# Two graph layers in one kernel: other block bounds, and the last two spans of each layer in an order of their own

## The chip, the core and the metric

The kernel runs on one core of one Trainium2 chip. The metric is the device time of one execution in microseconds (us), the median of five runs. A separate execution was taken with the hardware profiler. Engines are named as the profile names them: PE is TensorE (PEld its weight loads), DVE is VectorE, ACT is ScalarE, POOL is GpSimd, SP is SyncE, which here only issues DMAs. All data are float32.

## What is computed

There are N = 6250 nodes with D = 256 features and E = 106250 edges, sorted by destination; the last 6250 are the nodes' own loops. Each layer adds a per-edge message into the edge's destination and runs a small network on every node. The reference, cut to what matters (batch norm `_bn` and the weights are given as inputs):

```python
# layer 0
msg = relu(x[src] + edge_attr)
agg = segment_sum(msg, dst)
h = x + (x + agg)
f = gelu(_bn1(h) @ W1.T + b1) @ W2.T + b2
x = layernorm(x + _bn2(h + f))
# layer 1
m = gelu((x[src] + edge_attr) @ W1m + b1m) @ W2m + b2m
agg = segment_sum(m, dst) / max(deg, 1)
u = gelu(agg @ W1u + b1u) @ W2u + b2u
out = layernorm(x + _layer_norm(x + u, gamma, beta))
```

## The kernel before, in words

**Spans and blocks.** The edges are cut into 831 tiles of 128 (the last has 10), and eight tiles make a *span*: V = 104 spans, numbered 0 to 103, the last with seven tiles. A span has two groups of four tiles (`G = 4`), and a group two pairs. Nodes are cut into *blocks* of `SB = 256`: 25 of them, the last of 106. As the edges are sorted, a span touches a known range of nodes (`window[v]`, about 160 wide), so one or two blocks. `parts(v)` (L590) lists them, `first_span` and `last_span` say when a block opens and when it is full, and `shape(b)` (L604) gives its width, in how many halves H of n rows.

**Per span.** POOL gathers the source rows with one indirect DMA per tile (`gather`, L789) into one of five ring buffers (`RING = 5`, so POOL can run ahead until a ring is still in use). The edge rows are copied by ACT into PSUM (`lifted`, L825) and DVE adds them to the gathered ones (`add_to_gathered`, L833); ACT applies the function to a whole group (`activated`, L841). Each pair of tiles is then summed into 32 slots by matmuls with one-hot matrices made by DVE (`one_hots` L849, `into_slots` L868), ACT copies the slots out (`kept_slots` L884), and further matmuls with a second one-hot (`slot_nodes` L859) add them to the accumulator of the block (`into_blocks` L887).

**The product with W1m.** Layer 1 needs `edge_attr @ W1m`. PE turns a pair of tiles (`turned`, L800: transposes, then an ACT copy `eaT`) and multiplies them (`product`, L814). For the first group of each span this is done in layer 0, and the result stored to DRAM (`zst`, through the tile `z`, L1101 and L1110); layer 1 loads it in place of the edges. For the second group it is done in layer 1 (`load_1` L1237 loads its edges). The gathered table of layer 1 is not the node features but `proj`, their product with W1m, which the node part of layer 0 writes.

**Per block.** When a block is full its node part starts: a generator with stages, `nodes_0` (L972: batch norm, W1 and gelu, W2 with residual and statistics, normalization, transposes, projection and its write to `proj`) or `nodes_1` (L1170: mean, two halves of W1u and gelu, the residual's adds, W2u and statistics, first norm, second norm and output). `running` holds the generators under way and `advance` (L939) moves each by one stage. A norm's inverse root is an ACT square root and a DVE reciprocal (`inverted`, L959), and a square root and a gelu need different ACT tables. Every stage's PSUM comes from `node_work()` (L656), a pool with one buffer, `nodeP`; at the very end of a layer it takes `workP`, with four.

**The order.** The program is in manual schedule: each engine's queue holds its instructions in the order in which the code issues them. Step v (`step_0` L1080, `step_1` L1274) gathers span v, turns and multiplies, adds up span v-1, sums span v-2 into slots and span v-3 into blocks, and moves the generators by one stage each. After 104 steps `end_0` (L1114) or `end_1` (L1305) finishes what is left, with the last two blocks' generators moved together. Layer 1's first gather waits for every write to `proj`, since any edge may need any node. `end_0` also issues the first three spans' loads of layer 1 on SP, ahead of the last blocks' writes there.

## Time and profile before

| | us |
|---|---|
| median of 5 runs | 2770.07 |
| lowest and highest | 2761.28 and 2791.77 |
| the profiled execution | 2788.11 |
| its span, first to last instruction | 2786.2 |
| busy in it: PE, DVE, ACT, POOL | 2058.7, 1409.3, 1348.3, 1582.7 |
| last gather of layer 0 issued, first of layer 1 | 1311.1 and 1374.2 |
| last gather of layer 1 issued, end of the span | 2711.2 and 2786.2 |

A span's row in the list by order of time has: start, time, engine, line of the code, operation, what it writes and reads, shape, count, and in brackets how long the engine stood idle before it and what ended that. In the table by windows each row has the window, its length, then busy time (and count of instructions) of PE, PEld, DVE, ACT and POOL, the granted TensorE clock as a share of full speed, the DMA engines' share and GB/s. "remote" is a releaser that the profile could not name. Matmuls are pipelined and their ends are modelled.

### The profile page before, as it was taken

To read this page: it belongs to the slowest core of one execution; us is meant where nothing else is said; L and a number is where in the kernel's file an instruction comes from. 1 tells how busy PE (TensorE), PEld (TensorE's weight loads), DVE (VectorE), ACT (ScalarE), POOL (GpSimd) and SP (SyncE) were. 2 spreads that over 40 slices of the span, in tenths; PEclk is the share of its full clock that TensorE was granted. 3 is DMA by queue.
4 is the path that set the end of the run, shared out by engine and by line. 5 is a ranking of instruction groups with operands and counts; after the bars stand their busy time and mean duration, and the time that the engine had idled before them with its cause. 6 is when DMAs were issued, how large, how long until landed. Compare 5 with 4: busy or idle time off the path is not lost.

```text
span 2786.2 us, 37166 instructions
## 1 busy us (share of the span) xinstructions
PE 2058.7 (74%) x11784; PEld 1530.4 (55%) x11784; DVE 1409.3 (51%) x4130; ACT 1348.3 (48%) x2138; POOL 1582.7 (57%) x1671
## 2 busy tenths in 40 slices
PE   3778786788878878878726667776877678778786
PEld 2556565556655556656514555555655556555564
DVE  3545554455555555555313455444555546455455
ACT  1455554555555555555413444444454446445454
POOL 6565665566656656655255546555666566566550
PEclk7888998999999999999767888888999889898898
DMA  6677676667666767766445555555655456466550
GB/s 216 213 229 229 221 236 210 201 223 246 218 219 224 237 223 235 232 214 201 156 123 161 165 154 188 168 163 163 194 176 189 158 176 192 158 192 193 161 162 15
DMA packets 312069, 531.71 MB, mean 191 GB/s; under 512 B 36325, under 2 KB 231480, under 8 KB 311736
## 3 DMA queue, kind: packets, MB, share of 16 engines
q1 hardware_dynamic: 231416, 309.65, 33.5%
q0 software_dynamic: 79744, 217.71, 25.8%
q8 instruction: 97, 1.59, 0.2%
q10 hardware_dynamic: 704, 1.87, 0.2%
q14 instruction: 108, 0.88, 0.1%
HBM read 455.34 MB, written 73.75 MB: 190 GB/s over the span
## 4 chain that ended last, share of the span: by engine, by line
PE 20%; another core or an unknown queue 11%; issue 7%; DVE 6%; ACT 6%; DMA 2%; POOL 1%; ACTq 0%; SPq 0%; DVEq 0%; POOLq 0%
PE workP L819 8%; PE nodeP L1211 3%; PE acc L904 3%; PE slotP L876 2%; DVE ring L837 2%; ACT ring L845 2%; PE workP L806 2%; PE nodeP L1184 2%; DMA ring<-proj,src_sb 1%; DVE hot L854 1%; ACT workP L830 1%; ACT L961 1%; ACT eaT L811 1%; POOL ring L793 1%
## 5 line engine op out<-in xcount | busy, mean ns | idle before, releaser
L793 POOL DMA_INDIRECT ring<-proj,src_sb x831 | 790.6, 951 | 609.6 <-issue 275.2
L793 POOL DMA_INDIRECT ring<-in_x_dram,src_sb x831 | 790.2, 951 | 518.4 <-issue 257.6
L819 PE MATMUL workP<-w1m_sb,eaT 128*128 128x256 f32 x3324 | 891.7, 414 | 102.0 <-ACT eaT L811 67.7
L837 DVE TENSOR_TENSOR ring<-workP,ring 128x512 f32<-128x512 f32 x832 | 542.6, 683 | 562.5 <-remote 274.3
L819 PEld LDWEIGHTS workP<-w1m_sb,eaT 128*128 128x128 f32 x3324 | 653.3, 205 | 302.8 <-issue 91.1
L904 PE MATMUL acc<-hot,sums 128*128 128x160 f32 (+19 forms) x1360 | 268.3, 335 | 329.0 <-DVE hot L898 136.6
L845 ACT ACTIVATE ring<-ring 128x1024 f32<-128x1024 f32 x418 | 441.5, 1057 | 66.1 <-DVE ring L837 53.7
L904 PEld LDWEIGHTS acc<-hot,sums 128*128 128x128 f32 x1360 | 213.3, 220 | 372.5 <-ACT sums L885 124.4
L885 ACT COPY sums<-slotP 128x257 f32<-128x257 f32 (+1 forms) x208 | 77.2, 371 | 698.8 <-remote 355.0
L830 ACT COPY workP<-ea 128x512 f32<-128x512 f32 x624 | 343.5, 594 | 80.0 <-DVE ring L837 57.2
L811 ACT COPY eaT<-workP 128x512 f32<-128x512 f32 x416 | 230.4, 585 | 309.8 <-PE workP L806 127.2
L806 PE MATMUL workP<-ident,ea 128*128 128x128 f32 x1662 | 251.2, 286 | 143.6 <-DVE z L1101 71.2
L876 PE MATMUL slotP<-ring,hot 128*32 128x257 f32 (+1 forms) x3324 | 257.9, 407 | 77.3 <-remote 36.2
L806 PEld LDWEIGHTS workP<-ident,ea 128*128 128x128 f32 x1662 | 198.8, 146 | 204.0 <-DVE z L1101 92.5
L854 DVE TENSOR_SCALAR hot<-ramp,slot 128x32 f32<-128x32 f32 x1662 | 267.0, 260 | 0.0
L876 PEld LDWEIGHTS slotP<-ring,hot 128*32 128x32 f32 x3324 | 104.8, 113 | 201.3 <-issue 93.7
L1101 DVE COPY z<-workP 128x512 f32<-128x512 f32 x104 | 71.3, 686 | 198.4 <-PE workP L819 94.0
L917 DVE TENSOR_TENSOR degs<-degs,slotP 1x160 f32<-1x160 f32 (+24 forms) x170 | 36.3, 241 | 228.3 <-issue 89.1
L1194 ACT ACTIVATE uT<-uT,cols_sb 128x256 f32<-128x256 f32 (+1 forms) x100 | 44.6, 495 | 168.5 <-DVE uT L1189 128.6
L1110 DVE COPY z<-workP 128x512 f32<-128x512 f32 x104 | 71.4, 687 | 97.5 <-remote 48.1
L1184 PE MATMUL nodeP<-fT,w 128*128 128x256 f32 x368 | 97.8, 409 | 17.2 <-issue 8.5
L1211 PE MATMUL nodeP<-w2u_sb,uT 128*128 128x256 f32 x352 | 100.5, 450 | 0.0
(138 smaller groups left out, 1505.7 us busy)
## 6 DMA issues: line engine op xcount, KB each, us to landing
ea<-in_edge_attr_dram SPq DMA_DIRECT2D x103, 1024.0 KB
zst<-z SPq DMA_DIRECT2D x104, 512.0 KB
ea<-zst SPq DMA_DIRECT2D x104, 512.0 KB
ea<-in_edge_attr_dram SPq DMA_DIRECT2D x103, 512.0 KB
ring<-in_x_dram,src_sb POOLq DMA_INDIRECT x831
ring<-proj,src_sb POOLq DMA_INDIRECT x831
xb<-in_x_dram SPq DMA_DIRECT2D x24, 256.0 KB
x1d<-x SPq DMA_DIRECT2D x24, 256.0 KB
```

The costliest lines, as they stand in the source:

```text
L793: nc.gpsimd.indirect_dma_start(out=rings[v % RING][:n, g * G + j, :D], out_offset=None, in_=table, in_offset=bass.IndirectOffsetOnAxis(ap= ...
L806: nc.tensor.transpose(pe[:, j, k, :n], ea[:n, q + j, k * P : (k + 1) * P], ident[:n, :n])
L811: nc.scalar.copy(eaT[:, j:k, :, :n], pe[:, j:k, :, :n])
L819: nc.tensor.matmul(ph[:n, j, :], lhsT=eaT[:, j, k, :n], rhs=w1m_sb[:, k, :], start=(k == 0), stop=(k == KC - 1),)
L830: nc.scalar.copy(ps[:n, j:k, :], of[:n, q + j : q + k, :])
L837: nc.vector.tensor_add(r[:n, at + j : at + k, :D], ps[:n, j:k, :], r[:n, at + j : at + k, :D])
L845: nc.scalar.activation(at, at, func)
L854: nc.vector.tensor_scalar(hots[v][:n, j, :], ramp[:n, :SLOTS], slot[:n, t : t + 1], None, op0=ALU.is_equal,)
L876: nc.tensor.matmul(ps[q * SLOTS : (q + 1) * SLOTS, :width], lhsT=hot[:n, j, :], rhs=r[:n, j, :width], start=(i == 0), stop=(i == PAIR - 1 ...
L904: nc.tensor.matmul(acc[b][:, k, cols], lhsT=its[:, k * P : (k + 1) * P], rhs=at, start=(begins and k == 0), stop=(last_span[b] == v and k ...
L1184: nc.tensor.matmul(ps[:, o - i, :width], lhsT=w12[:, k, o * P : (o + 1) * P], rhs=mT[:, k, :width], start=(k == 0), stop=(k == KC - 1),)
L1211: nc.tensor.matmul(ps[:n, h, :], lhsT=uT[:, k, h * P : h * P + n], rhs=w2u_sb[:, k, :], start=(k == 0), stop=(k == UC - 1),)
```

## The change

It has six parts.

- **Bounds.** The blocks are no longer multiples of 256. The last two get 160 and 96 nodes (`LAST`), the first takes the rest of 106, and 23 of 256 lie between: 26 blocks. A block of 160 has two halves of 80 rows. Indices `b * SB` become `bounds[b]` throughout, and the halves' columns `h * P` become `h * n`.
- **The last two steps.** `step_0` and `step_1` run for spans 0 to 101. The last two (c and d in the code) are in `end_0` and `end_1`, with `advance(list(running))` at places of their own. The very last span is added, activated and summed into slots pair by pair (`arriving`), with a stage of every running generator between the pairs.
- **Products of the last spans.** Spans 102 and 103 have both groups multiplied in layer 0 (`stored_products`), in half-steps that `fill` places between the other work and, for the rest, after the last node part; the second groups go to a new DRAM tensor `zst1`, and layer 1 loads them from there. So layer 1 has no products for these two spans, and layer 0's last two steps have none in their usual place.
- **Banks and roots.** The last two blocks' stages take PSUM from `workP` or from the accumulators' pool, and their inverse root is a DVE add and a power on POOL (`inverted` with `last`).
- **Loads and gathers.** The source indices are loaded in two pieces, the first of 64 columns. A span's gathers are issued with the short tile first, and this tile, which has 10 edges, is gathered with 127 rows in layer 0 and 120 in layer 1. Two spans' loads of layer 1 are issued ahead of the last node parts, the third after them.
- **Small.** `invert` (the reciprocal of the degrees) is called at the end of `full_1` and no longer at the end of the step; code that was not used is gone.

The diff, cut to its core:

```diff
--- before.py
+++ after.py
...
+LAST = (160, 96)
...
+LATE = 2
+FIRST = 64
...
     c.update(
...
+    bounds = [0, (N - sum(LAST)) % SB]
+    while bounds[-1] < N - sum(LAST):
+        bounds.append(bounds[-1] + SB)
+    for width in LAST:
+        bounds.append(bounds[-1] + width)
+    if bounds[1] == 0:
+        bounds.pop(0)
+    blocks = len(bounds) - 1
     V = len(window)
 
     def parts(v):
 
         lo, hi = window[v]
         return [
-            (b, max(lo, b * SB), min(hi, (b + 1) * SB))
-            for b in range(lo // SB, (hi - 1) // SB + 1)
+            (b, max(lo, bounds[b]), min(hi, bounds[b + 1]))
+            for b in range(blocks)
+            if bounds[b] < hi and lo < bounds[b + 1]
         ]
...
     def shape(b):
 
-        width = min(SB, N - b * SB)
+        width = bounds[b + 1] - bounds[b]
         H = -(-width // P)
-        assert width == H * min(width, P)
-        return width, H, min(width, P)
+        assert width % H == 0
+        return width, H, width // H
 
     def rows_of(ap, b):
...
             return psw.tile([P, 2, D], F32, name="workP")
 
-        draining = []
-
         def node_work():
-            return work() if draining else psn.tile([P, 2, D], F32, name="nodeP")
+            return psn.tile([P, 2, D], F32, name="nodeP")
+
+        def acc_work():
+            return psa.tile([P, KC, SB], F32, name="acc")
 
...
 
-            nc.sync.dma_start(out=src_sb, in_=src)
+            nc.sync.dma_start(out=src_sb[:, :FIRST], in_=src[:, :FIRST])
+            nc.sync.dma_start(out=src_sb[:, FIRST:], in_=src[:, FIRST:])
...
 
-        def gather(v, table):
-            for g in range(GROUPS):
-                for j, n in enumerate(tiles_of(v, g)):
-                    t = v * SPAN + g * G + j
-                    nc.gpsimd.indirect_dma_start(
-                        out=rings[v % RING][:n, g * G + j, :D],
-                        out_offset=None,
-                        in_=table,
-                        in_offset=bass.IndirectOffsetOnAxis(ap=src_sb[:n, t : t + 1], axis=0),
-                    )
+        def gather(v, table, least=0):
+            counts = tiles_of(v, 0) + tiles_of(v, 1)
+
+            for j in sorted(range(len(counts)), key=lambda j: counts[j]):
+                t, n = v * SPAN + j, max(counts[j], least)
+                nc.gpsimd.indirect_dma_start(
+                    out=rings[v % RING][:n, j, :D],
+                    out_offset=None,
+                    in_=table,
+                    in_offset=bass.IndirectOffsetOnAxis(ap=src_sb[:n, t : t + 1], axis=0),
+                )
 
...
+        def activated_pair(v, g, q, func):
+            at = g * G + q
+            for j, k, n in runs(tiles_of(v, g)[q : q + 2]):
+                r = rings[v % RING][:n, at + j : at + k, :D]
+                nc.scalar.activation(r, r, func)
+
...
+        def slots_of(v, width, ps, its):
+
+            hot, r = hots[v], rings[v % RING]
+            counts = tiles_of(v, 0) + tiles_of(v, 1)
+            for j in its:
+                n, q, i = counts[j], j // PAIR, j % PAIR
+                nc.tensor.matmul(
+                    ps[q * SLOTS : (q + 1) * SLOTS, :width],
+                    lhsT=hot[:n, j, :], rhs=r[:n, j, :width],
+                    start=(i == 0), stop=(i == PAIR - 1 or j + 1 == len(counts)),
+                )
+
+        def slot_bank():
+            return pss.tile([P, 2 * D], F32, name="slotP")
...
-        def inverted(mv, n, H):
-
-            nc.scalar.activation(mv[:n, :H, 1], mv[:n, :H, 1], AF.Sqrt, bias=eps[:n, :])
-            nc.vector.reciprocal(mv[:n, :H, 1], mv[:n, :H, 1])
+        def inverted(mv, n, H, last):
+
+            var = mv[:n, :H, 1]
+            if last:
+
+                nc.vector.tensor_scalar(var, var, EPS, None, op0=ALU.add)
+                nc.gpsimd.tensor_tensor(var, var, root[:n, :H], op=ALU.pow)
+            else:
+                nc.scalar.activation(var, var, AF.Sqrt, bias=eps[:n, :])
+                nc.vector.reciprocal(var, var)
 
...
+        def nodes_0(b, acc, xb, deg, bank, last):
...
             running.append(gen)
 
-        def full_0(v):
+        def full_0(v, bank=node_work, last=False):
             for b in into_blocks(v, acc, opened_0, degs):
-                begun(b, nodes_0(b, acc.pop(b), xbs.pop(b), degs.pop(b)))
+                begun(b, nodes_0(b, acc.pop(b), xbs.pop(b), degs.pop(b), bank, last))
...
+        def added(v, g):
+
+            for q in range(0, len(tiles_of(v, g)), 2):
+                add_to_gathered(v, g, q, lifted(v, g, q, eas[v, g]))
+
+        def arriving(v, width, func, ready, between):
+
+            starts = [
+                (g, q) for g in range(GROUPS) for q in range(0, len(tiles_of(v, g)), 2)
+            ]
+            ps = slot_bank()
+            slot_nodes(v)
+            rows = ready(*starts[0])
+            for i, (g, q) in enumerate(starts):
+                add_to_gathered(v, g, q, rows)
+                if i + 1 < len(starts):
+                    rows = ready(*starts[i + 1])
+                activated_pair(v, g, q, func)
+                at = g * G + q
+                between()
+                slots_of(v, width, ps, range(at, at + len(tiles_of(v, g)[q : q + 2])))
+            kept_slots(v, ps, width)
+
+        def stored_products(v, g, to):
+
+            counts = tiles_of(v, g)
+            z = ep.tile([P, G, D], F32, name="z", bufs=2)
+            for q in range(0, len(counts), 2):
+                pair, eaT = turned(v, g, q, eas[v, g])
+                yield
+                ph = product(pair, eaT)
+                for j, k, n in runs(pair):
+                    nc.vector.tensor_copy(z[:n, q + j : q + k, :], ph[:n, j:k, :])
+                yield
+            for j, k, n in runs(counts):
+                nc.sync.dma_start(
+                    out=to[:n, j * D : k * D], in_=z[:n, j:k, :].rearrange("p j d -> p (j d)")
+                )
+
+        def all_products():
+            for v in (V - 2, V - 1):
+                yield from stored_products(v, 0, zst[v])
+                yield from stored_products(v, 1, zst1[v - (V - LATE)])
+
         def end_0():
 
...
+
+            a, b, c, d = V - 4, V - 3, V - 2, V - 1
+            rest = all_products()
+
+            def fill(count):
+                for _ in range(count):
+                    next(rest, None)
+
+            gather(c, x)
+            one_hots(b)
+            full_0(a - 1)
+            activated(a, 1, AF.Relu)
+            added(b, 0)
+            slot_nodes(a)
+            kept_slots(a, into_slots(a, D + 1), D + 1)
+            advance(list(running))
+            added(b, 1)
+            activated(b, 0, AF.Relu)
+            activated(b, 1, AF.Relu)
+            full_0(a)
+            slot_nodes(b)
+            kept_slots(b, into_slots(b, D + 1), D + 1)
+            advance(list(running))
+
+            gather(d, x, P - 1)
+            one_hots(c)
+            full_0(b)
+            added(c, 0)
+            advance(list(running))
+            activated(c, 0, AF.Relu)
+            added(c, 1)
+            fill(1)
+            advance(list(running))
+            activated(c, 1, AF.Relu)
+            fill(1)
+            slot_nodes(c)
+            kept_slots(c, into_slots(c, D + 1), D + 1)
+            advance(list(running))
+            one_hots(d)
+            full_0(c, work, True)
+
+            def between():
+                advance(list(running))
+                fill(1)
+
+            arriving(d, D + 1, AF.Relu, lambda g, q: lifted(d, g, q, eas[d, g]), between)
+            full_0(d, acc_work, True)
+            for v in range(AHEAD - 1):
                 load_1(v)
...
+            while running:
+                advance(list(running))
+                fill(1)
+            for _ in rest:
+                pass
+            load_1(AHEAD - 1)
 
 
         UC = w1u_sb.shape[2] // P
...
+            if v < V - LATE:
+                load_edges(v, [1], eas[v, 1])
+                return
+            for j, k, n in runs(tiles_of(v, 1)):
+                nc.sync.dma_start(
+                    out=eas[v, 1][:n, j:k, :].rearrange("p j d -> p (j d)"),
+                    in_=zst1[v - (V - LATE), :n, j * D : k * D],
+                )
 
         def opened_1(b):
...
-        def full_1(v):
+        def full_1(v, bank=node_work, last=False):
             for b in into_blocks(v, acc_1, opened_1):
-                begun(b, nodes_1(b, acc_1.pop(b), x1s.pop(b), degs_1.pop(b), invs.pop(b)))
+                its = acc_1.pop(b), x1s.pop(b), degs_1.pop(b), invs.pop(b)
+                begun(b, nodes_1(b, *its, bank, last))
+            invert()
 
         def step_1(v):
...
+
+            a, b, c, d = V - 4, V - 3, V - 2, V - 1
+            gather(c, proj)
+            first, second = turned(b, 1, 0, eas[b, 1]), turned(b, 1, 2, eas[b, 1])
+            one_hots(b)
+            full_1(a - 1)
+            activated(a, 1, AF.Gelu)
+            added(b, 0)
+            advance(list(running))
+            first = product(*first)
+            slot_nodes(a)
+            kept_slots(a, into_slots(a, D), D)
+            add_to_gathered(b, 1, 0, first)
+            activated(b, 0, AF.Gelu)
+            add_to_gathered(b, 1, 2, product(*second))
+            activated(b, 1, AF.Gelu)
+            full_1(a)
+            advance(list(running))
+            slot_nodes(b)
+            kept_slots(b, into_slots(b, D), D)
+
+            gather(d, proj, P - 8)
+            one_hots(c)
+            advance(list(running))
+            full_1(b)
+            added(c, 0)
+            activated(c, 0, AF.Gelu)
+            advance(list(running))
+            added(c, 1)
+            activated(c, 1, AF.Gelu)
+            advance(list(running))
+            slot_nodes(c)
+            kept_slots(c, into_slots(c, D), D)
+            advance(list(running))
+            one_hots(d)
+            full_1(c, work, True)
+            arriving(
+                d, D, AF.Gelu, lambda g, q: lifted(d, g, q, eas[d, g]),
+                lambda: advance(list(running)),
+            )
+            full_1(d, acc_work, True)
+            while running:
+                advance(list(running))
 
         begin()
         for v in range(AHEAD):
@@ -1334,11 +1456,11 @@
         load_w(w2t_sb, w2t)
         slots_of_edges()
         beside = {1: norms, 2: weights_of_layer_1, 3: strays, 6: join_weights}
...
+        for v in range(V - LATE):
             step_0(v)
             beside.get(v, lambda: None)()
         end_0()
...
+        for v in range(V - LATE):
             step_1(v)
         end_1()
```

## The prediction

> **What bounds the kernel now.** I read the busy times first, then the two places where the gathers have ended and nothing new arrives (the tail of each layer), by windows and in order of time, and last the opening of layer 1.
>
> ```profile
> span 2786.2 us, 37166 instructions
> PE 2058.7 (74%) x11784; PEld 1530.4 (55%) x11784; DVE 1409.3 (51%) x4130; ACT 1348.3 (48%) x2138; POOL 1582.7 (57%) x1671
> ```
>
> No engine is full over the span, so what the change is worth must be read at its places. Layer 0's tail, in order of time:
>
> ```profile
> 1310.18 0.89 POOL L793 DMA_INDIRECT ring<-in_x_dram,src_sb  x1 [0.30 <-issue]
> ...
> 1367.18 0.42 DVE L1038 TENSOR_TENSOR y<-workP,rows_sb 106x256 f32<-106x256 f32 x1 [0.23 <-PE workP L1034]
> ...
> 1374.21 0.98 POOL L793 DMA_INDIRECT ring<-proj,src_sb  x1 [63.13 <-DMA proj<-y]
> ...
> 1433.18 0.95 POOL L793 DMA_INDIRECT ring<-proj,src_sb  x1 [0.30 <-issue]
> 1441.42 0.69 DVE L837 TENSOR_TENSOR ring<-workP,ring 128x512 f32<-128x512 f32 x1 [45.35 <-remote]
> ```
>
> The last gather of layer 0 is issued by 1311.1; layer 1's first waits 63 us for the last row of `proj`. Then POOL issues 48 gathers without a break and DVE stands 45 us until just after the last. The opening of layer 0 looks alike (POOL without a break from 5.6 to 55.7, DVE's z copy resumes at 61.5). I take it that an opening lasts as long as five rings take to fill, which the change leaves alone: what the tail gains or loses goes on one for one.
>
> The windows of both tails:
>
> ```profile
> 1315.20:1334.20 19.00, 18.84 (x120) 14.39 (x119) 14.09 (x41) 12.64 (x21) 0.00 (x0) 1.00 0.18 70
> 1334.20:1347.60 13.40, 10.46 (x61) 5.47 (x60) 6.40 (x25) 7.82 (x16) 0.00 (x0) 0.68 0.15 59
> 1347.60:1367.60 20.00, 16.23 (x75) 13.39 (x74) 7.27 (x20) 5.89 (x11) 0.00 (x0) 0.79 0.63 210
> ...
> 2713.60:2722.90 9.30, 8.04 (x53) 6.17 (x52) 6.73 (x22) 7.21 (x10) 0.00 (x0) 1.00 0.00 1
> 2722.90:2731.90 9.00, 8.11 (x53) 6.30 (x53) 6.33 (x21) 7.65 (x12) 0.00 (x0) 1.00 0.05 16
> 2731.90:2747.40 15.50, 11.53 (x70) 6.38 (x68) 7.66 (x23) 6.91 (x15) 0.00 (x0) 0.82 0.03 10
> 2747.40:2766.50 19.10, 14.79 (x59) 12.44 (x59) 8.62 (x27) 8.14 (x15) 0.00 (x0) 0.77 0.00 0
> 2766.50:2778.70 12.20, 4.90 (x17) 3.58 (x15) 10.26 (x31) 1.18 (x4) 0.00 (x0) 0.78 0.08 24
> 2778.70:2786.20 7.50, 0.00 (x0) 0.00 (x0) 0.00 (x0) 0.00 (x0) 0.00 (x0) 0.50 0.18 56
> ```
>
> After the length come PE, PEld, DVE, ACT and POOL busy, then the clock. Layer 0's tail is steps 102 and 103 (19.0 us), the hand-written end (13.4), then two blocks' node chains side by side (20.0). Layer 1's is the same: 18.3, 15.5, 31.3, and 7.5 for the last output. POOL is idle in both: these stretches are bound by the order in which the three compute queues wait for each other.
>
> **How I cost the new order.** I write each engine's queue down in the order of the changed code and let each instruction start when its queue and its operands are there, with durations from rows: one_hots 1.25, a pair's add 0.69, a pair's lift 0.58, a half's activation 1.06, slots 1.07, slot copy 0.38, product 1.99, a stage of 16 weight matmuls 4.0, table load 1.28, sqrt 0.29, the two x adds and statistics 2.6. The same working puts the before's add of span 101 at 8.7 us after 2713.6; its row says
>
> ```profile
> 2722.27 0.69 DVE L837 TENSOR_TENSOR ring<-workP,ring 128x512 f32<-128x512 f32 x1
> ```
>
> Two things set the pace: `nodeP` has one buffer, and `advance(list(running))` moves two blocks' generators through it one behind the other, with the edges' adds queued behind the nodes' DVE work.
>
> **Layer 0's tail, zero at 1315.2** (DVE done with step 101's z). Blocks 23 (256 nodes), 24 (160) and 25 (96) end at spans 100, 102 and 103.
> - Span 101: one_hots 1.25, degs 0.30, two adds 1.29, hot 0.30; block 22's sqrt with its table and its scaling are in the way until 4.85; adds to 6.15, degs, hT and hot to 7.5, the next one_hots to 8.75.
> - Span 102: slots to 8.4, block 22's transposes and copy to 10.0, block 23's W1 behind it in the one bank to 12.0, its gelu to 12.95, lifts to 14.05, adds to 15.8. PE's projection of block 22 ends at 16.1, y at 16.9, block 23's second matmuls (3.4) at 20.3, its adds and statistics at 23.0; only then the second half's adds to 24.3, activation 25.4, slots 26.5, transposes 27.5, accumulation 29.0, fT 29.8.
> - Span 103: pair 0 to 31.7, block 24's table and gelu to 33.7, second matmuls 37.1, adds and statistics 39.8, a moved z copy 40.5, pair 2's add 41.2, eps, power and scaling 43.2, pair 3 to 44.6; a moved product sits ahead of the last slots, 46.3; slot copy 46.7, accumulation 47.5, fT 48.2.
> - Drain: block 24's projection to 49.7, block 25's W1 and gelu 51.4, second matmuls 53.1, a moved product and z copy 55.8, power and scaling 57.4, transposes, behind another product 60.0, projection 61.0, y 61.5.
>
> So y ends at 1376.7, against 1367.6: **+9**. The landing (6.3 us from issue to gather here) may shorten, since two spans' loads instead of three stand before it: 0 to -3, I take -1. The last two spans' sixteen tiles of products are covered by this tail and by the 10 us before the first gather lands; without that cover the 8 pairs would cost 8 x 2.5 = 20 us of PE. On SP the loads of spans 0 and 1 go ahead of the last writes, as three did before.
>
> **Layer 1's tail, zero at 2713.6.** Span 101's products and adds to 7.85, activation 8.95; block 23's mT at 8.8; block 22's 16 matmuls to 12.05 and statistics to 13.95; block 23's first matmuls wait for the bank, 14.85, their DVE part 15.75; one_hots 17.3. Block 22's sqrt (with table) and DVE work to 21.4; block 23's second matmuls again wait for the bank, 22.35; block 25's reciprocal to 24.6; adds 25.9, activation 27.0; block 22's last sqrt and scaling 29.5, block 23's adds 30.85; second half's adds 32.15; block 23's matmuls to 34.9, statistics 36.8, sqrt and DVE work 41.2; one_hots 42.3. Four pairs with block 24's stages between them: 43.75, 48.3, 49.75, 54.05; its matmuls to 55.4, statistics 57.3; block 25's mT 57.75. Its drain, beside block 24's last two stages, ends the scaling at 73.1. In the before the last scaling ends 65.1 after the same zero:
>
> ```profile
> 2778.25 0.41 DVE L966 TENSOR_SCALAR y<-y,mv 106x256 f32<-106x256 f32 x1
> ```
>
> That is **+8**, with 7.5 for the output behind both. The products removed there (4 pairs, 10 us of PE) were off this path: DVE and the bank set it.
>
> **Small parts.** The source indices come in two pieces; gathers start at 5.63, 4.9 us after that load's issue. The piece has 1/13 of the bytes: bounds 0 and -2.9, I take -1.5, because POOL's run sets the opening. `pow` on POOL has no row. Nearest are POOL's 0.10 (memset) and 1.38 (its longest gather); I take 1.0, nearer to the gather, because it is computed in software; six stand on the path: -5 to +2. The ACT table loads of blocks 24 and 25 go; they are counted in the chains above. Each gather of the odd tile with 127 or 120 rows instead of 10, the sorted gathers and the reciprocal inside `full_1`: 0, POOL's issue being 0.95 for any of them; without that cover one gather, 1.25.
>
> The row has a table load at 1.28. The Trainium skill (ScalarE: Activation LUTs, What ACT_TABLE_LOAD costs) gives 2.66 for a switch with its drain; by that the before's four tail loads would be worth 5.5 us more than here, but the sqrt follows 0.02 us behind the load in this trace.
>
> The longest POOL row is 1.38. The Trainium skill (GPSIMD Engine Reference, Instruction dispatch) says that the first call of a freshly loaded kernel on that engine pays about 6 us; that speaks against the power there and would add 5 us once, an estimate that no row here shows.
>
> **Sum.** 9 - 1 + 8 - 1.5 = +14.5. The profiled execution took 2788.1 (span 2786.2 and 1.9 around it), 18 above the median of the five runs, 2770.1, and inside their range (2761 to 2792). On the median: **2784**, own range 2769 to 2797.
>
> **Rivals.**
> 1. *The order packs as meant.* Layer 1's tail needs 44 us of DVE (39.6 now, less 6, plus 10.6 for the extra block), layer 0's 41 us of PE. At 88%, PE's share in steps 102 and 103, they last 50 and 47 instead of 65 and 52.4: -20, with the start **2748**. For it: every engine has 30 to 40% of the tails free. Against it: the single bank.
> 2. *Layer 1's opening stalls less,* because PE comes into it from moved products. The 45 us lie there: 2784 - 45 = **2739**. Against it: layer 0's opening stalls alike, and PE idles some 10 us first in either kernel.
> 3. *Slower: PE at half clock in the tails.* Twelve matmuls at 1362.4 took 4.70, 0.39 each, not 0.25; on the two paths stand some 110 (blocks 23 to 25 with 80, four products with 32) and 88 (three stages of 16, five of 8), 0.14 x 198 = 28: **2812**. It decides when the tails' granted clock falls to about 0.6; the windows show 0.68 to 1.00.
>
> **How the numbers follow.** Forecast 0.56, rivals 0.15, 0.12 and 0.17. A measurement of this kernel can tell about 1% (28 us) from no change. Faster by more: rival 2 with 0.10, 0.06 of rival 1 and 0.01 of the forecast, 0.17. Slower by more: rival 3 with 0.16 and 0.03 of the forecast, 0.19. Between: 0.64. The range takes rival 1 and the near half of the others: 2740 to 2808.
>
> **What would show it.** Right: last y of layer 0 some 60 us after step 101, layer 1's first gather about 8 us later after the last gather than the 63 here; the last scaling 73 us after step 101 of layer 1; an opening with 40 or more gathers on end. Wrong: block 25's accumulation within 45 us of step 101 in layer 1 (rival 1), a stall in the opening under 20 us (2), matmuls of 0.4 us in the tails (3), or a power over 2 us.

## The result, and the profile after

The ratio of the changed kernel to the one before is 1.009, with a 95% interval of 1.0067 to 1.0112. On the 2770.07 us of before that is +25 us (19 to 31), or 2795; the forecast was 2784, +14. This is inside the 1% that counts as no change, on the slow side of it, with the upper end of the interval just outside. The medians over all executions (2820.5 and 2781.2) stand further apart, because the ratio leaves out executions that took over 1.5% more than the fastest of their kernel (35 of the changed kernel's here, and in the experiments a single one of the kernel before, of 10098 us). The profiled execution of after took 2797.85 us; its page begins with

```profile
span 2796.0 us, 37385 instructions
PE 2081.4 (74%) x11850; PEld 1541.0 (55%) x11850; DVE 1420.1 (51%) x4167; ACT 1360.1 (49%) x2156; POOL 1589.7 (57%) x1677
```

There is a little more work on each engine (PE 22.7 us, DVE 10.8, POOL six powers), but every engine idles for a quarter of the span or more, so this says nothing of where the end moved. The tails have to be read. Layer 0's tail and the opening of layer 1, in order of time:

```profile
1309.68 2.56 POOL L810 DMA_INDIRECT ring<-in_x_dram,src_sb  x1 [2.77 <-ACT sums L916]
...
1321.08 0.69 DVE L1126 COPY z<-workP 128x512 f32<-128x512 f32 x1 [1.79 <-remote]
1381.22 0.42 DVE L1054 TENSOR_TENSOR y<-acc,rows_sb 96x256 f32<-96x256 f32 x1 [0.17 <-PE acc L1050]
1386.00 1.03 POOL L810 DMA_INDIRECT ring<-proj,src_sb  x1 [8.32 <-ACT eaT L828]
...
1426.32 1.29 DVE L854 TENSOR_TENSOR ring<-workP,ring 128x512 f32<-128x512 f32 x2 [20.80 <-ACT ring L862]
1440.73 0.69 DVE L854 TENSOR_TENSOR ring<-workP,ring 128x512 f32<-128x512 f32 x1 [13.12 <-remote]
```

The z copy at 1321.08 is step 101's, whose end is the zero of the prediction. In the profile before it is

```profile
1314.61 0.68 DVE L1110 COPY z<-workP 128x512 f32<-128x512 f32 x1
```

The last y ends 59.9 us after this zero (1381.64 less 1321.77), and 52.3 in the profile before (1367.60 less 1315.29). The first gather of layer 1 follows y by 4.4 us, 6.6 before. The first row is the last span's short tile gathered with 127 rows: 2.56 us where the others take 0.95.

The last two rows are of layer 1's opening. VectorE stood there 45.35 us in one piece before, and now 20.80 and 13.12, 11 us less; TensorE's longest stand fell from 49.5 to 17.2 us, and 40 gathers instead of 48 were issued on end.

Windows of layer 1's tail (columns as in the prediction's):

```profile
2727.00:2746.00 19.00, 11.33 (x36) 8.79 (x40) 8.16 (x22) 8.39 (x12) 0.00 (x0) 0.64 0.04 14
2766.00:2783.30 17.30, 8.85 (x32) 6.03 (x30) 10.59 (x34) 1.92 (x6) 2.80 (x4) 0.68 0.05 13
2783.30:2796.00 12.70, 0.00 (x0) 0.00 (x0) 0.00 (x0) 0.00 (x0) 0.00 (x0) 0.50 0.04 12
```

In the last window, behind the last scaling, no engine has any work. It is 12.7 us long and was 7.5. Layer 1's tail, in order of time:

```profile
2708.41 1.04 PE L823 MATMUL workP<-ident,ea 128*128 128x128 f32 x8
...
2727.68 3.60 PE L1278 MATMUL nodeP<-fT,w 128*128 128x256 f32 x8 [4.53 <-DVE y L1319]
...
2739.47 6.42 PE L1305 MATMUL nodeP<-w2u_sb,uT 128*128 128x256 f32 x16 [6.36 <-DVE y L1298]
...
2767.40 0.69 PE L936 MATMUL acc<-hot,sums 128*128 128x96 f32 x4 [0.46 <-ACT sums L916]
...
2782.28 0.55 POOL L975 TENSOR_TENSOR mv<-mv,root 96x1 f32<-96x1 f32 x1 [1.51 <-DVE mv L974]
2782.86 0.41 DVE L982 TENSOR_SCALAR y<-y,mv 96x256 f32<-96x256 f32 x1 [0.73 <-POOL mv L975]
```

The first row is span 101's transposes, which start the stretch that the prediction costed. From there the last scaling ends after 74.9 us (2708.41 to 2783.27); before it was 64.8 (2713.83 to 2778.66), counted from

```profile
2713.83 1.04 PE L806 MATMUL workP<-ident,ea 128*128 128x128 f32 x8
```

The two waits of PE in the middle (4.53 and 6.36) end when DVE has read the one `nodeP` bank: the pace-setter that the prediction named.

What SyncE waited for at the end shows why the last window grew (who waited, for whom, us in total, times, longest):

```profile
SPq L1522 <- PEq L1522: 7.3, 2, 6.8
```

L1522 is the end of the program, where all queues meet. In the profile before, the same wait is short:

```profile
SPq L1400 <- PEq L1400: 0.7, 2, 0.5
```

The records of POOL's own queue name the late one: behind the last power stand a branch, a semaphore instruction of 1.9 us and a drain of 7.0 us (2787.9 to 2794.9). Before, POOL's last work was the last gather, so the same pair (1.6 and 5.9 us) ran from 2713.2 to 2720.7, with 58 us of the other engines' work still to come.

### The profile page after: what moved, and what is told of

Same layout as the page of the kernel before. It is cut to its first block, busy times and chain, and to the rows that moved or that the text cites. A ratio compares the mean times of both kernels' runs of the same rounds, so it can differ in the third digit from the quotient of the medians.

```text
span 2796.0 us, 37385 instructions
## 1 busy us (share of the span) xinstructions
PE 2081.4 (74%) x11850; PEld 1541.0 (55%) x11850; DVE 1420.1 (51%) x4167; ACT 1360.1 (49%) x2156; POOL 1589.7 (57%) x1677
## 4 chain that ended last, share of the span: by engine, by line
PE 21%; another core or an unknown queue 9%; issue 7%; ACT 6%; DVE 6%; DMA 1%; POOL 1%; ACTq 0%; DVEq 0%; POOLq 0%
PE workP L836 8%; PE nodeP L1305 3%; PE slotP L897 3%; PE acc L936 3%; PE workP L823 2%; PE nodeP L1278 2%; ACT ring L862 2%; DVE ring L854 1%; DMA ring<-proj,src_sb 1%; ACT workP L847 1%; ACT L977 1%; DVE uT L1283 1%; ACT eaT L828 1%; DVE hot L877 1%
## 5 line engine op out<-in xcount | busy, mean ns | idle before, releaser
L936 PE MATMUL acc<-hot,sums 128*128 128x161 f32 (+17 forms) x1376 | 270.3, 335 | 286.4 <-DVE hot L930 112.7
L1288 ACT ACTIVATE uT<-uT,cols_sb 128x256 f32<-128x256 f32 (+3 forms) x104 | 45.8, 487 | 181.3 <-DVE uT L1283 154.9
L949 DVE TENSOR_TENSOR degs<-degs,slotP 1x161 f32<-1x161 f32 (+17 forms) x172 | 36.4, 239 | 189.3 <-issue 78.9
L1305 PE MATMUL nodeP<-w2u_sb,uT 128*128 128x256 f32 (+1 forms) x376 | 112.4, 465 | 6.4 <-DVE y L1298 6.4
L1278 PE MATMUL nodeP<-fT,w 128*128 128x256 f32 (+1 forms) x384 | 97.9, 398 | 24.9 <-issue 13.2
```

The costliest lines, as they stand in the source:

```text
L936: nc.tensor.matmul(acc[b][:, k, cols], lhsT=its[:, k * P : (k + 1) * P], rhs=at, start=(begins and k == 0), stop=(last_span[b] == v and k ...
L1278: nc.tensor.matmul(ps[:, o - i, :width], lhsT=w12[:, k, o * P : (o + 1) * P], rhs=mT[:, k, :width], start=(k == 0), stop=(k == KC - 1),)
L1305: nc.tensor.matmul(ps[:n, h, :], lhsT=uT[:, k, h * n : (h + 1) * n], rhs=w2u_sb[:, k, :], start=(k == 0), stop=(k == UC - 1),)
```

## Experiments

The experiments ran in four groups, each on one chip beside the kernel before. There the kernel before took 2178 to 2183 us and not 2781 (more on this at the end), and runs of one kernel agreed within 0.4%. Each ratio is to the kernel before on the same chip; 0.001 is 2.2 us. Marks in us are from the profile of each run, and repeat to some 2 us (layer 0 is the same in the last version and in edges_first, and its gap is 36.8 and 39.0). The *gap* is from the end of layer 0's last gather to the start of layer 1's first; the *tail* is from the end of layer 1's last gather to the end of the span.

**Before and after again.** Both unchanged.

> The kernel before, unchanged, for a profile beside those of the experiments, whose chip ran every kernel in about four fifths of the time of the first comparison (the kernel before 2178 us against 2781). If the marks of the first profiles hold there: 63 us from the last gather from x to the first from proj, 75 us from the last gather to the end. If the stretches without any work on TensorE and VectorE (the waits put down to another core or an unknown queue, 9 per cent of the chain) are what is gone, the two stretches fall to some 40 and 50 us, and no stand-still of over 20 us is left at the layers' openings.

> The change, unchanged, on the same chip as the kernel before. Theory (the loss lies in the tails: the order of the node stages in layer 1's tail, and GpSimd's closing sequence behind its last power): ratio 1.006 to 1.011, of it 5 to 7 us between the last scaling and the end, and the rest in layer 1's tail and in the gap between the layers, with the two layers' gather stretches within 3 us of those of the kernel before. Rival (the bodies differ, by the other phase of blocks against spans or by the extra block): the stretches from first to last gather are longer by 5 us or more each.

The kernel before: 2181.8 us, ratio 0.9998 (0.9988 to 1.0008). After: 2202.7, ratio 1.0091 (1.0076 to 1.0107), the same loss on quite another level of time. In the kernel before, the gap is 39.1 us here (63.1 in the first profile) and the tail 47.3 (75.0), and VectorE's longest stand in an opening is 11.5: the first of the two expectations came out near its second case. The tops of the two pages, before first:

```profile
PE 1874.6 (86%) x11784; PEld 1443.2 (66%) x11784; DVE 1417.5 (65%) x4130; ACT 1338.1 (62%) x2138; POOL 1577.8 (73%) x1671
PE 1883.8 (86%) x11850; PEld 1448.6 (66%) x11850; DVE 1430.8 (65%) x4167; ACT 1349.0 (61%) x2156; POOL 1592.1 (72%) x1677
```

As the groups on POOL show (kernel before), the gathers set the pace of both layers here:

```profile
L793 POOL DMA_INDIRECT ring<-in_x_dram,src_sb x831 | 787.7, 948 | 255.7 <-issue 141.9 <-DMA ring<-in_x_dram,src_sb 32.6 <-PE slotP L876 11.0
```

255.7 us of idle time are 831 times 0.31, the pause between any two gathers. The 831 gathers of a layer stand on end, one every 1.25 us; the first comparison's profile has 518.4 there. So here a gain or loss in a tail goes on one for one, and the marks can be put side by side:

| us | predicted | first comparison | experiments' chip |
|---|---|---|---|
| layer 0: zero to last y | +9 | 52.3 to 59.9, +7.6 | 56.4 to 61.4, +5.0 |
| last y to first gather | -1 | 6.6 to 4.4, -2.2 | 6.3 to 4.4, -1.9 |
| layer 1: span 101's transposes to last scaling | +8 | 64.8 to 74.9, +10.1 | 65.9 to 73.8, +7.9 |
| last scaling to end | 0 | 7.6 to 12.8, +5.2 | 6.9 to 12.9, +6.0 |
| first gather | -1.5 | 5.63 to 4.88, -0.75 | 5.34 to 4.70, -0.64 |
| gather of the short tile, layer 0 | 0 | 0.89 to 2.56, +1.7 | 0.88 to 2.56, in the first row |
| sum | +14.5 | +21.7 | +16.4 |
| the ratio's | | +25 (19 to 31) | +20 |

In the last column the short tile is gathered after the zero, so its 1.7 us lie inside the first row and are not added again.

The table holds only the stretches that the prediction costed, and what lies between them changed too. The two profiles on the experiments' chip differ by 27.9 us (spans 2173.4 and 2201.3): 16.4 in the table and 11.5 in the two layers from their first gather to the zero. The profiled execution of the kernel before was 6.6 us under its median, that of the change 0.5 above, so the medians (+21) leave some 4 or 5 us of the 11.5. The first comparison's two profiles differ by only 9.8 us: layer 1 from its first gather to the zero is 17 us shorter in the change's, with VectorE's shorter stand (11 us) in it. There the sum of the table is not the difference of the profiles, and that it comes near the ratio's +25 shows little.

The rival's longer bodies came too, by its own bound of 5 us: the stretches from the first to the last gather grew by 6.5 and 5.9 us. In each, 2.5 us are the usual gather's 949 ns against 946, which also differs between runs of one group; in layer 0, 1.7 are the short tile. In layer 1 the gathers of over 1.0 us rose from 16 to 33, some 3 us.

**The order alone.**

```diff
-LAST = (160, 96)
+LAST = (106,)
```

> The change with the block bounds of the kernel before (multiples of 256, the last block 106 columns), everything else as in the change. Theory A (the new order of the last steps sets the loss, by the one nodeP bank and by generators moved one behind the other): the loss stays, ratio to the kernel before 1.005 to 1.015; the last scaling still ends 70 us or more after the last step's first transposes, and some 12.5 us, not 7.5, pass from the last scaling to the end of the span. Theory B (the two small blocks cost it, by one more block's chain of node stages): ratio 0.997 to 1.003, and the tail is some 8 us shorter than with the new bounds.

Ratio 1.0101 (1.0086 to 1.0117). The last scaling ends 73.4 us after span 101's transposes and 12.7 before the end. Theory A holds as far as this run goes: the bounds of the blocks are not what costs, the rest of the change is.

**Roots on ScalarE in the ends.**

```diff
-                nc.vector.tensor_scalar(var, var, EPS, None, op0=ALU.add)
-                nc.gpsimd.tensor_tensor(var, var, root[:n, :H], op=ALU.pow)
+                nc.scalar.activation(var, var, AF.Sqrt, bias=eps[:n, :])
+                nc.vector.reciprocal(var, var)
```

> The change with ScalarE's square root and VectorE's reciprocal in the ends, where it has an add on VectorE and a power on GpSimd. Theory C (the last power makes GpSimd the last engine: its closing sequence, a 1.9 us semaphore instruction and a 7.0 us drain, ran from 2714.9 to 2720.7 in the shadow before and runs from 2785.6 to 2795.3 with nothing beside it now): from the last scaling to the end of the span 7.5 us again and not 12.8; the six roots on the path cost 1 to 2 us more each, so the last scaling is 3 to 10 us later, and the time is that of the change within 5 us. Rival (the output's transfer of 96 rows is what takes 12.8 us): 12.8 us again.

Ratio 1.0074 (1.0060 to 1.0088), 3.7 us under the change, which the intervals do not tell apart. The profile does: 5.7 us from the last scaling to the end (12.9 in the change), with the same transfer of 96 rows, and SyncE's last wait is short:

```profile
SPq L1522 <- PEq L1522: 1.0, 2, 0.9
```

The roots cost layer 1's tail 2.8 us more (76.6 to the last scaling, 73.8 in the change), a little less than expected. Theory C holds.

**Four banks for the ends' node stages.**

```diff
-            full_1(a - 1)
+            full_1(a - 1, work)
...
```

and so for `a` and `b`, in both layers.

> The change with the node stages of every block that is completed in the ends in the four workP banks instead of the one nodeP bank. Theory A1 (the one bank sets the pace of the tails): in layer 1 the last scaling ends 62 to 70 us after the last step's first transposes, where the change has 74.9; the stretch between the last gather from x and the last y falls from 61.9 to 52 to 58 us; the time falls by 8 to 16 us. Rival A2 (VectorE, with the edges' adds ahead of the node stages in its queue, sets the pace): both stay within 3 us, and so does the time.

Ratio 1.0047 (1.0033 to 1.0060), 9.6 us under the change, with intervals that do not meet. The last scaling ends 66.6 us after span 101's transposes, and layer 0's stretch from the last gather to the last y falls from 36.2 to 31.6 (the 61.9 that I had set the expectation against was the first comparison's). In the rows of TensorE the waits for the bank are gone:

```profile
2118.78 1.89 PE L1278 MATMUL workP<-fT,w 128*128 128x256 f32 x8
...
2121.60 1.99 PE L1278 MATMUL workP<-fT,w 128*128 128x256 f32 x8
```

The second half of L1278 follows 0.9 us behind the first, with the slots between them; in the change it waited 4.53, in both of its profiles. Theory A1 holds. Layer 1's tail is then as long as before's (65.9), up to the last scaling.

**Banks, and the last roots alone on ScalarE.** As banks, with in `nodes_1`

```diff
             mv = deviations(y, n, H)
             yield
-            inverted(mv, n, H, last)
+            inverted(mv, n, H, False)
```

> The change with the ends' node stages in the four workP banks, as in the run before, and with the last inversion of layer 1's last two blocks by ScalarE's root and VectorE's reciprocal, so that GpSimd has its last power some 10 us ahead of the last scaling. Theory C (GpSimd's closing sequence is bare at the end): from the last scaling to the end 5 to 7.5 us where banks alone has 12.7, the last scaling 1 to 4 us later, the time 3 to 6 us under that of banks alone, ratio about 1.002. Rival: the roots on ScalarE, with a table load of 1.28 us ahead, cost what the closing gives, and the time is that of banks alone.

Ratio 1.0033 (1.0020 to 1.0045), 3 us under banks, not told apart. The end took 9.8 us, not 5 to 7.5: POOL's last power ended at 2175.3, its drain ran to 2187.3, and the roots put the last scaling 2.5 us later after the last gather. POOL's closing takes some 12 us from its last work on, so it is hidden here only if that work is so far ahead of the end.

**The second halves' products back in layer 1.**

```diff
             for v in (V - 2, V - 1):
                 yield from stored_products(v, 0, zst[v])
-                yield from stored_products(v, 1, zst1[v - (V - LATE)])
...
-            added(c, 1)
+            for q in range(0, len(tiles_of(c, 1)), 2):
+                add_to_gathered(c, 1, q, product(*turned(c, 1, q, eas[c, 1])))
```

> The change with the second halves' products of the last two spans made in layer 1 again, as the other spans' are, and not in the gap. Theory (the products made in the gap lie beside other work and cost nothing there, and what they save in layer 1's tail is the PE work of 14 products of some 0.8 us): the gap is within 2 us of the change's, layer 1's tail is 3 to 10 us longer, and the time as much. Rival (they hold up the gap's node stages on TensorE and VectorE): the gap is 4 us or more shorter, and the time the same or less.

Ratio 1.0121 (1.0106 to 1.0137), 6.5 us above the change; the intervals just touch. The gap between the layers is 39.7 us (change 40.6), and the last scaling ends 54.6 us after the last gather (change 49.0). So the moved products cost the gap 1 us at most, and save 5 to 6 us in layer 1's tail.

**Gathers paced by the one-hot matrices.**

```diff
             counts = tiles_of(v, 0) + tiles_of(v, 1)
+            if v - 2 in hots:
+                nc.gpsimd.tensor_copy(pace, hots[v - 2][:, 0, 0:1])
```

> The change with one copy of 128 numbers on GpSimd ahead of each span's gathers, that reads the one-hot matrix of two spans before: GpSimd can no longer issue the gathers of several spans in one unbroken run (40 at each layer's opening, 15 or 16 at eleven to thirteen places). Theory F (in an unbroken run of gathers, from some 11 us on, the profile shows almost no packet on the queues marked instruction, and TensorE, ScalarE and VectorE stand still until the run ends: they lack instructions): the stand-still at the openings (61 us in layer 0, 40 to 50 us in layer 1) shrinks by more than half, instruction packets appear in the openings, and the time falls by 40 to 100 us. Rival (the engines wait there for rows and edge data that the DMA engines, busy at 70 to 90 per cent, cannot bring sooner): the openings last as long and the time is that of the change within 10 us, or up to 30 us more for the 208 copies.

Ratio 1.0187 (1.0174 to 1.0201), 21 us above the change. The test missed its object: on these chips no stand-still of that kind is in any profile, with or without the copies (VectorE's longest in an opening is 14 us). Theory F falls as it was put, since in the kernel before again 831 gathers stand on end with 99 packets of the instruction queues among them, and the engines work. What the run shows is the rival's last clause: where POOL sets the pace, the copies (202 more instructions on POOL) lengthen the two bodies, by 8.6 and 5.4 us in the profiles, 14 of the 21.

**All costs taken back.** The edits of banks and of sqrt_in_ends, and

```diff
-            gather(d, x, P - 1)
+            gather(d, x)
...
-            gather(d, proj, P - 8)
+            gather(d, proj)
...
                 begun(b, nodes_1(b, *its, bank, last))
-            invert()
...
             advance(late)
+            invert()
```

> The change's order and bounds, with each cost that the runs so far have shown taken back: the four workP banks for the ends' node stages, roots on ScalarE, the last spans' first gathers with their own 10 rows (not 127 and 120), and the inverse degrees at the end of a step of layer 1 as before. If the account is whole, the sum over the change's 2202.7 is 9.6 less for the banks, some 4.5 less for the closing sequence with the roots' own cost off, 1.9 less for the two short gathers (2.57 us against 0.95 us in layer 0) and up to 3 less for the gathers of over 1 us that lie beside the inverses: about 2183, ratio 0.998 to 1.003. If a cost is missing from the account, the ratio stays above 1.004.

Ratio 1.0009 (1.0000 to 1.0018), 2180.7 us, where 2183 was worked out. The sum comes out to 2 or 3 us, and with these four costs off the order does neither good nor harm. The sum of four terms is shown here, and not each of them: against banks the gap is 4.5 us longer (41.1 and 36.7) and the tail 6.0 shorter (49.7 and 55.8). Gathers of over 1.0 us in layer 1 are 21, not 33.

**The last span's edges first.**

```diff
             def between():
-                advance(list(running))
-                fill(1)
+                advance(running[:1])
```

and the same in layer 1.

> The kernel all_mended with one more edit: between the pairs of the last span only the oldest generator is moved, not all of them, and no products are made there in layer 0. In the runs with the banks the last span's slots were complete 22.6 us after the last gather, in the kernel before 9.7 us, and the rest of the chain took 20 us against 31. Theory D (the node stages put between the pairs hold up the last span more than they help the blocks before it): slots 11 to 15 us after the last gather, last scaling 35 to 40 us after it (before 40.4, banks 43.1), the time 3 to 8 us under all_mended, ratio 0.996 to 1.000. Rival (what is not done between the pairs comes afterwards, since the last two blocks' stages then run together on TensorE and VectorE): last scaling 43 us or more after the last gather, time as all_mended or above.

Ratio 0.9991 (0.9982 to 1.0000), 4 us under all_mended (the intervals just touch), in the expected size but not where I expected it: the last span's slots ended 23.4 us after the last gather (11 to 15 expected), the last scaling 44.1 (35 to 40), as in all_mended. The gap shrank from 41.1 to 39.0, no more than marks repeat to, so where the 4 us lie is not shown. Theory D failed for layer 1. The last gather ends at 2128.00, and DVE's adds of the last two spans show why:

```profile
2124.12 1.29 DVE L854 TENSOR_TENSOR ring<-workP,ring 128x512 f32<-128x512 f32 x2
2130.18 1.28 DVE L854 TENSOR_TENSOR ring<-workP,ring 128x512 f32<-128x512 f32 x2
2140.53 0.67 DVE L854 TENSOR_TENSOR ring<-workP,ring 128x512 f32<-128x512 f32 x1
```

The first two are span 102's, whose gathers were issued by 2119.3; the third is span 103's first. In the kernel before, whose last gather ends at 2126.10, the last span's last adds are

```profile
2131.18 1.00 DVE L837 TENSOR_TENSOR ring<-workP,ring 128x512 f32<-128x512 f32 x2
```

So the lateness is there before the first pair, whatever stands between the pairs. On DVE's queue these adds stand behind node stages that wait for other engines; the last run below moves them.

**Layer 0's end alone.** Layer 0's end as in all_mended; the bounds, the products and layer 1's end (`end_1`) as in the kernel before:

```diff
-LAST = (160, 96)
+LAST = (106,)
...
-                yield from stored_products(v, 1, zst1[v - (V - LATE)])
...
-        for v in range(V - LATE):
+        for v in range(V):
             step_1(v)
         end_1()
```

> Layer 0's end as in all_mended, and layer 1's end, its products and the block bounds as in the kernel before. Theory (the loss is in layer 1's tail and its closing; layer 0's end with four banks is no worse than before's): the gap between the layers 36 to 39 us (39.1 before), the tail within 1.5 us of the 47.3 before, ratio 0.9975 to 1.0005. Rival (the small last blocks are what made the gap shorter in the runs with banks): gap 40 us or more and ratio 1.001 or more.

Ratio 1.0036 (1.0024 to 1.0048), gap 44.7 us, tail 49.2: the rival's numbers came. With blocks of 256 and 106 at the end, the new order of layer 0 has a gap 3.6 us longer than in all_mended, with 160 and 96 (41.1). That the bounds do it is likely and not shown, since layer 0 also has fewer products here: the bounds alone made the gap 1.5 us longer (order_alone 42.2, change 40.6), the products alone 0.9 shorter (products_late). Of the 3.6, 2.6 lie behind the last y: the first gather follows it by 8.3 us, in all_mended by 5.7.

**Adds ahead of the node stages.** As edges_first, with layer 1's last two steps in this order:

```diff
             one_hots(c)
-            advance(list(running))
             full_1(b, work)
             invert()
             added(c, 0)
-            activated(c, 0, AF.Gelu)
             advance(list(running))
+            activated(c, 0, AF.Gelu)
             added(c, 1)
             activated(c, 1, AF.Gelu)
             advance(list(running))
             slot_nodes(c)
             kept_slots(c, into_slots(c, D), D)
-            advance(list(running))
             one_hots(d)
+            advance(list(running))
             full_1(c, work, True)
             invert()
+            advance(running[:-1])
+            advance(running[:-1])
-            arriving(d, D, AF.Gelu, ..., lambda: advance(running[:1]))
+            arriving(d, D, AF.Gelu, ..., lambda: None)
```

> The kernel edges_first with layer 1's last two steps in another order: the last two spans' adds are put on VectorE's queue ahead of the node stages, the stages of the block completed three spans earlier are finished before the last span's adds, and nothing is moved between the last span's pairs. In edges_first the adds of the last span but one ran 2124.1 to 2131.5, though its rows had landed by some 2121, and the last span's first add ran at 2140.5, 12.5 us after the last gather: on VectorE's queue they stand behind node stages that wait for TensorE and ScalarE. Theory E (the place in VectorE's queue is what is late): first add of the last span within 6 us of the last gather, its slots within 13 us (before 9.7, edges_first 23.4), last scaling 32 to 40 us after the last gather (edges_first 44.1, before 40.4), time 4 to 10 us under edges_first, ratio 0.995 to 0.9975. Rival (the chain of the last two blocks' stages on TensorE and VectorE is as long wherever it begins): the last span is early, the last scaling still 42 us or more behind the last gather, time within 3 us of edges_first.

Ratio 0.9978 (0.9969 to 0.9988), 2176.6 us: the only version that is faster than both kernels by its interval, by 0.2% of before and 1.1% of the change. The last scaling ends 39.5 us after the last gather (before 40.4, change 49.0), at the slow edge of the forecast. Against edges_first it gained 2.8 us, under the 4 to 10 expected, and the intervals do not tell the two apart; in the profiles the tail is 4.7 us shorter (45.1 and 49.8). Its last gather ends at 2129.39:

```profile
2127.70 1.29 DVE L854 TENSOR_TENSOR ring<-workP,ring 128x512 f32<-128x512 f32 x2 [2.01 <-ACT workP L847]
2143.17 1.28 DVE L854 TENSOR_TENSOR ring<-workP,ring 128x512 f32<-128x512 f32 x2
```

Span 102's last adds (the first row) came 4 us earlier against the last gather, but the last span's first add (the second) is still 13.8 us behind it (under 6 expected), and its slots 20.5 (under 13): the two stages that I put ahead of it have 16 matmuls of 4.2 us and two rounds of statistics in them. Theory E is half shown: with the adds moved up the last scaling came 4.6 us earlier after the last gather (39.5 and 44.1), and how far it could go stays open.

## Why the prediction was right, and which terms were wrong

- **What bounds the tails: right.** The single bank was worth 9.6 us (banks), and DVE's queue, with adds behind waiting node stages, is seen in the rows of edges_first. "What would show it" came as put: the last y 59.9 us after step 101 (some 60), the last scaling 74.9 after span 101's transposes (73), 40 gathers on end in the opening (48 before, though the sum took the opening as equal). One item missed: layer 1's first gather came 3 us later than the 63, not 8. The zero sits at step 101's z, and the last gathers ran later against it than before.
- **Layer 0's tail, +9 and -1:** +7.6 and -2.2, on the experiments' chip +5.0 and -1.9. Right in kind, 3 to 5 us too slow in size.
- **Layer 1's tail, +8:** +10.1 and +7.9. The 2 us between the two are no more than marks repeat to. In both profiles one stage of 16 matmuls took longer than the 4.0 taken: 6.42, in a window with the clock at 0.64, and 5.85; the other two took 3.62 and 3.68 in both.
- **"7.5 for the output behind both": the term that failed.** It was taken as the output's transfer, equal in both kernels. The end waits for the last queue to close, and with the power as POOL's last work that queue is POOL's: +5.2 and +6.0, shown by sqrt_in_ends. I had costed how long the power takes (1.0; it took 0.55 to 0.90) and not what stands behind it on its engine.
- **The first call.** The first power took 0.73 us. The 6 us that the Trainium skill (GPSIMD Engine Reference, Instruction dispatch) gives for a first call is not seen. Adding its 5 us would have come nearer to the total, for a wrong reason.
- **The odd tile's gather, 0:** 127 rows took 2.56 us and not 0.95, +1.7.
- **"The products removed there were off this path": wrong.** products_late puts all four pairs back, in the new order, and shows 5 to 6 us for them. The sum did not suffer, since the chain was costed without them. Their cover in the gap was judged rightly.
- **Start, -1.5:** -0.75 and -0.64, inside the bounds.
- **`invert`, 0:** some 3 us of longer gathers in layer 1 are not in the sum. The Trainium skill (SBUF — State Buffer, Who interferes with whom) says that some VectorE instructions lock a port that GpSimd needs. In the repeated change 17 of layer 1's 33 gathers of over 1.0 us overlap the maximum, reciprocal or minimum of `invert`, and 42 of the other 798; for the one-hots the shares hardly differ (13 of 33, 271 of 798). In the seven runs on these chips with `invert` inside `full_1`, 12 to 24 such long gathers overlap it; in the five with `invert` at the end of the step, 1 to 5, though as many gathers overlap it there. The banks, the roots, the products and the bounds vary among these runs; only the rows of the short tile, one gather of a layer, always go with the place. So the place of `invert` most likely makes these gathers longer; that a locked port is the reason is argued and not shown.
- **Rivals.** 1 fell: block 25's accumulation came 59 us after the zero in layer 1 (2767.40), not within 45. 2 did not come in the time, but in part in the first comparison's two profiles: the longest stand fell from 45 to 20.8 us, just above its sign of 20, and both stands together are 11 us shorter. That an opening lasts as long as five rings take to fill (40 gathers) fits the change and not the 48 of before. Why it shortened is open, and on the experiments' chip there is no such stand to shorten. 3 came in one of three stages of 16 matmuls (0.40 each) and in the last one of 8 (3.70 in all, 0.46 each), with the clock at 0.64 to 1.00 over the tails' windows; but the last 24 of the kernel before took 0.35 each too.

The forecast was on the right side of 1% because the two large terms were right within 4 us. That what was left out (7 us for the closing and the short gather, and some 4 in the two layers' bodies) was partly offset by 3 to 5 us too much for layer 0 is luck.

## What to carry to other kernels

Ask of every instruction that moves to another engine not only what it costs there, but whether it becomes that engine's last work, and what its queue still has to do behind it. The hand-written order gained nothing here while the stages shared one PSUM bank and while adds whose data had landed stood in a queue behind stages that wait; give the stages banks first, then read the rows of the adds against the landing of their data. Repeating both kernels where one engine sets the pace of the body made a difference of 1% legible term by term.

## What the runs showed of the hardware that I had not expected

- GpSimd closes this program, which issues indirect gathers, with a semaphore instruction and a drain behind its last work. They took 1.6 and 5.9 us in the six runs whose short tiles are gathered with 10 rows, and 1.9 and 7.0 in the eight with 127 and 120, with or without powers.
- A gather of 127 rows took 2.56 us on POOL, of 128 rows 0.95, of 120 rows 0.99, of 10 rows 0.88.
- The kernel before took 2781 us in the first comparison and 2178 to 2183 on the four chips of the experiments. The work is the same: DVE is busy 1409 and 1418 us, POOL 1583 and 1578, PE 2059 and 1875 at a granted clock of 0.873 and 0.947. What differs is idle time. In the first profile it was mostly put down to "remote" on ACT (355 us before the slot copies) and DVE (274 before the adds) and to "issue" on POOL (533), and the openings' stand-stills are part of it; on the other chips these are gone. What caused it is open: the run that was meant to show it ran where it does not occur.
